# Pairwise products of 4096 rows: when, and through which queue, the input is loaded

## The chip, the cores and the metric

The kernel runs on 1 core of one Trainium2 chip. Its time is device microseconds of one execution; the number given is the median of several. Five engines take part: VectorE (DVE in the profile), ScalarE (ACT), GpSimd (POOL), SyncE (SP) and TensorE (PE, here only a relay for a semaphore). Each has its own stream of instructions. Transfers between HBM and the on-chip memory run on 16 DMA engines; SyncE and GpSimd each have a queue that feeds them (q1 and q0 in the profile).

## What is computed

The input has 4096 rows of 256 numbers. For each row, all products of two of its elements with the first index not above the second are written out in order: 256 x 257 / 2 = 32896 numbers per row.

```python
d = inputs.shape[1]
dot = jnp.einsum('bi,bj->bij', inputs, inputs)
iu, ju = jnp.triu_indices(d)
return dot[:, iu, ju]
```

All in 32-bit floats: 4.19 MB are read and 538.97 MB written.

## The kernel before

The 128 partitions hold 32 input rows each. Two rows of every partition make a *unit* (`each` = 512 floats, 2 KB per partition, 256 KB in all); there are 16 units, all kept in the tile `x`. A *pass* covers two units, so a loop of 8 passes (`h` from 0 to 7) covers the input. Each pass has six *pieces* (`p` from 0 to 5), three for each unit. A piece is a third of the 32896 output columns for the two rows of a unit: about 10.9 thousand floats by 2 rows by 128 partitions, 10944 or 11008 KB.

Pieces are computed into two places, `o0` and `o1`, in turn. VectorE copies the unit to `xv` and `xp` (line 209) and multiplies one element by the elements that follow it (line 230); GpSimd does the same for its share of the piece (line 315). The shares are cut so that GpSimd's part is estimated at 19.4 us. When both are done, SyncE issues one store of the whole piece (line 343). Its landing frees the place (`free0`, `free1`), VectorE waits for that before it starts the next piece there (lines 217 and 220), and it lets GpSimd start with `go`. So two stores can be in the queue: while one is being written, the piece for the other place is computed.

The first two pieces (`AHEAD`) are computed ahead of the loop by VectorE and ScalarE, and GpSimd does nothing then. Piece 0 goes out in five stores of growing size (`FIRST`), which raise `head`; TensorE waits for all five and then raises `free0`. VectorE and GpSimd then wait for the remaining early loads, and enter the loop with piece 2. At the end of a pass each engine computes the first two pieces of the next one.

The input comes in two ways. `NEAR` (line 383) are three loads of SyncE over all partitions: unit 0, units 1 and 2, and units 3 to 7. VectorE and ScalarE start when the first has landed. `LATE` are the units 8 to 15, by GpSimd in two turns: in pass 2 the units 8, 9, 12 and 13, in pass 3 the units 10, 11, 14 and 15. The issues stand in GpSimd's stream behind its part of pieces 2 and 3 (`late`, lines 281 and 274), five loads after each, and behind piece 5 it waits for them, with one drain after the second turn.

A late load takes 14 partitions, every ninth one (`COMB` = 9), and two runs of 4 KB in each; a last one takes the two partitions that are left. Between two loads stands a *mark*: a tiny load of 2 rows to a tile `marks` that nobody reads. One mark of 5 rows (`FORE`) comes first, and one of 14 (`AFT`) ends a turn. A load of 14 rows and a mark of 2 take 16 rows together.

Of the kernel before, what the change touches and what calls it, by code (L numbers as in the profile page):

```python
# [12 lines left out]
P = 128  # L13
# [1 line left out]
REPEAT = 2  # L15
PIECES = 3
EDGE = 32
NEAR = [(0, 1), (1, 3), (3, 8)]
LATE = {2: (8, 12), 3: (10, 14)}
TURNS = {2: range(5), 3: range(5, 10), 5: ()}  # L20
UNITS = 2
COMB = 9
FORE, AFT = 5, 14
MARK = 64
PLACES = 2
SETS = 2
# [39 lines left out]
def interleave(block: list) -> list:  # L66


    sets, k = [], 0
    for left in range(SETS, 0, -1):  # L70
        share = -(-len(vector_ops(block[k:])) // left)
        end = k
        while end < len(block) and len(vector_ops(block[k : end + 1])) <= share:
            end += 1
        if left == 1:
            end = len(block)
        sets.append(vector_ops(block[k:end]))
        k = end
    order, last = [], {}
    for step in range(max(map(len, sets))):  # L80
        for s, ops in enumerate(sets):
            if step < len(ops):
                order.append((*ops[step], last.get(s)))
                last[s] = len(order) - 1 if ops[step][1] == 2 else None
    return order


def schedule(order: list) -> dict:


    waits = {}
    for k, (*_, before) in enumerate(order):
        if before is not None and before > max(waits.values(), default=-1):
            waits[k] = max(before, k - 2)
    return waits
# [21 lines left out]
def window(ap: bass.AP, free: list) -> bass.AP:  # L117
    return bass.AP(ap.tensor, ap.offset, [list(ap.ap[0]), *free])
# [3 lines left out]
def kernel(  # L122
# [15 lines left out]
    nc = tc.nc  # L138
    n, d = x.shape
    width = out.shape[1]  # L140
    each, groups = REPEAT * d, n // (P * REPEAT)
# [8 lines left out]
    x_in = x.rearrange("(p g) d -> p (g d)", p=P)  # L150
# [5 lines left out]
    xt = pool.tile([P, passes, rounds * each], F32, name="x")  # L156
    xv = pool.tile([P, each + 1], F32, name="xv")
    marks = pool.tile([P, 2, 2 * MARK], F32, name="marks")
# [4 lines left out]
    def semaphore(name: str):  # L163
        return ctx.enter_context(nc.semaphore(name))

    free = [semaphore(f"free{k}") for k in range(PLACES)]
    head, v_done, a_done, go = (semaphore(s) for s in ("head", "v_done", "a_done", "go"))
    loaded = [semaphore(f"loaded{k}") for k in range(len(NEAR))]
    far, marked = semaphore("far"), semaphore("marked")
    teeth = P // COMB  # L170
    rest = P - COMB * teeth

    def take(engine, sem, value: int):
        engine.wait_ge(sem, value).then_inc(sem, -value)  # L174
# [7 lines left out]
    def blocks(p: int, ahead: bool):  # L182

        lo, hi = spans[p % PIECES]
        cuts = [lo, *(FIRST if ahead and p == 0 else []), hi]
        for a, b in zip(cuts, cuts[1:]):
            block = runs(d, a, b)
            if ahead:
                k = split(block)
                yield a - lo, b - lo, block[:k], block[k:], lo  # L190
            else:
                k = next(k for k in range(len(block)) if gpsimd_time(block[k:]) <= BUDGET * 1e3)
                yield a - lo, b - lo, block[k:], block[:k], lo
# [73 lines left out]
                else:  # L267
                    nc.scalar.sem_inc(a_done, 1)

    flat = xt.rearrange("p h d -> p (h d)")  # L270

    def mark(lo: int, hi: int):
        of = window(x_in[lo:hi], [[2 * MARK, 2], [1, MARK]])
        nc.gpsimd.dma_start(marks[lo:hi, :, :MARK], of).then_inc(marked, 16)  # L274

    def load_late(units: tuple, k: int):
        one, two = units
        rows = slice(k, k + COMB * (teeth - 1) + 1, COMB) if k < COMB else slice(P - rest, P)
        free = [[(two - one) * each, 2], [1, UNITS * each]]
        to, of = (window(ap[rows, one * each :], free) for ap in (flat, x_in))  # L280
        nc.gpsimd.dma_start(to, of).then_inc(far, 16)  # L281
        if k < COMB:
            mark(FORE + rest * k, FORE + rest * (k + 1))
        else:
            mark(FORE + rest * k, FORE + rest * k + AFT)

    def late(h, p: int):
        for turn, (when, units) in enumerate(LATE.items()):
            with nc.gpsimd.If(h == when):
                if TURNS[p]:  # L290
                    for k in TURNS[p]:
                        if turn == k == 0:
                            mark(0, FORE)
                        load_late(units, k)
                else:
                    nc.gpsimd.wait_ge(far, 16 * (turn + 1) * (COMB + 1))
                    nc.gpsimd.wait_ge(marked, 16 * ((turn + 1) * (COMB + 1) + 1))
                    if turn + 1 == len(LATE):
                        nc.gpsimd.drain()

    def gpsimd(h, pieces: range, ahead: bool):

        done = turns = 0
        for p in () if ahead else pieces:
            place = places[p % PLACES]
            ((_, _, block, _, lo),) = blocks(p, False)
            turns += 1
            nc.gpsimd.wait_ge(go, turns)
            order = interleave(block)
            waits = schedule(order)  # L310
            counted = {len(order) - 1, *waits.values()}
            number = {k: done + 1 + c for c, k in enumerate(sorted(counted))}
            for k, ((i, j, at, length), m, _) in enumerate(order):
                at -= lo
                ins = nc.gpsimd.tensor_tensor(  # L315
                    place[:, :, at : at + m * length],
                    window(xv[:, j:], [[d, REPEAT], [1, m], [1, length]]),
                    window(xv[:, i:], [[d, REPEAT], [1, m], [0, length]]),
                    ALU.mult,
                )  # L320
                if k in waits:
                    ins._wait_ge(g_own, number[waits[k]])
                if k in counted:
                    ins.then_inc(g_own, 1)
            done += len(counted)
            nc.gpsimd.wait_ge(g_own, done).then_inc(g_done, 1)  # L326
            if p in TURNS:
                late(h, p)
            if (p + 1) % PIECES == 0:
                nc.gpsimd.sem_inc(x_read, 1)  # L330
        if turns:
            nc.gpsimd.sem_inc(g_own, -done)
            nc.gpsimd.sem_inc(go, -turns)
# [14 lines left out]
    def settle(done: int, ahead: bool = False):  # L348
        nc.sync.sem_inc(v_done, -done)
        nc.sync.sem_inc(a_done if ahead else g_done, -done)  # L350

    def all_pieces(engine, pieces_of):
        done = pieces_of(0, range(AHEAD), True)
        if engine is nc.vector:
            nc.vector.sem_inc(v_own, -done)
        elif engine is nc.sync:
            settle(done, True)
        if engine is not nc.sync:
            for sem in loaded[1:]:
                engine.wait_ge(sem, 16)  # L360
        kind = engine.engine
        with nc.Fori(
            0,
            passes,
            engines=OrderedEngineSet([kind]),
            head_slot={kind: 0} if engine is not nc.sync else {},
        ) as h:
            done = pieces_of(h, range(AHEAD, PASS), False)
            with engine.If(h < passes - 1):
                nxt = nc.s_assert_within(h + 1, 0, passes - 1)  # L370
                if engine is nc.vector:
                    nc.vector.sem_inc(v_own, -vector(nxt, range(AHEAD), False, done))
                elif engine is nc.sync:
                    settle(sync(nxt, range(AHEAD), False, done) - done)
                else:
                    pieces_of(nxt, range(AHEAD), False)
            if engine is nc.sync:
                settle(done)
        if engine is nc.vector:
            nc.vector.sem_inc(v_own, -done)  # L380

    for (lo, hi), sem in zip(NEAR, loaded):
        nc.sync.dma_start(flat[:, lo * each : hi * each], x_in[:, lo * each : hi * each]).then_inc(sem, 16)

    nc.vector.memset(xv[:, each:], 0.0)  # L385
    for engine in (nc.vector, nc.scalar):
        engine.wait_ge(loaded[0], 16)
# [4 lines left out]
    for engine, pieces_of in ((nc.vector, vector), (nc.gpsimd, gpsimd), (nc.sync, sync)):  # L392
        all_pieces(engine, pieces_of)
# [32 lines left out]
```

## Time and profile before

| | |
|---|---|
| median of 3 runs | 1269.0 us (1268.93 to 1269.31) |
| the profiled execution | 1268.93 us, its span 1267.1 us |
| VectorE busy | 795.2 us (63% of the span) |
| GpSimd busy | 789.6 us (62%) |
| ScalarE busy | 29.2 us (2%) |
| bytes moved | 543.26 MB, mean 429 GB/s |
| GpSimd's late loads | 20, issued from 367.6 to 558.9 us, 23.6 us of GpSimd with their 21 marks |
| such a load of 112 KB, issue to landing | 22.4 us in the median, 48.3 us for the last ones |
| a store of 10944 KB, issue to landing | 33.8 us in the median |
| start of VectorE's first copy | 3.66 us |
| piece 1 enters SyncE's queue | about 37 us |
| VectorE and GpSimd start piece 2 | 41.88 us |

The profile shows one execution. Its span runs from the first instruction to the last. For the DMA engines it gives the share of time in which they moved packets, as a mean of the 16, by stretches. In a stretch that is not much longer than a packet this share jitters, and can be above 1, since a packet is put to the stretch in which it starts. The trace also holds a record of each packet: its start, its duration, its size and its queue, though not the number of its engine.

### The profile page before, as it was taken

How to read it: one execution, taken by the hardware profiler on the slowest of the kernel's cores; microseconds unless marked ns; L12 is line 12 of the kernel's file. 1: busy time of each engine (PE TensorE's matmuls, PEld its weight loads, DVE VectorE, ACT ScalarE, POOL GpSimd, SP SyncE). 2: the span in 40 equal slices, each digit the busy share in tenths (PEclk: the TensorE clock that was granted, in tenths of full speed). 3: DMA queues.
4: the chain of work that ended last, by engine and by line, in shares of the span. 5: the costliest groups of instructions: out<-in, count | busy, mean ns of one | idle time of the engine just before them, and what ended most of it. 6: DMA issues, size and time to landing. Idle time of an engine off the chain costs nothing. (4 is left out here: it accounts for less than half of the span.)

```text
span 1267.1 us, 3025 instructions
## 1 busy us (share of the span) xinstructions
DVE 795.2 (63%) x1197; ACT 29.2 (2%) x79; POOL 789.6 (62%) x1073
## 2 busy tenths in 40 slices
DVE  8856846667475674756747666486655866468560
ACT  8000000000000000000000000000000000000000
POOL 0467664776578765787655775567656675566750
DMA  9999999999999999999999999999999999999998
GB/s 380 394 444 420 442 439 424 441 423 442 422 436 431 430 426 440 428 426 432 437 429 439 429 435 430 436 442 424 438 429 437 439 427 439 426 438 431 435 440 349
DMA packets 16215, 543.26 MB, mean 429 GB/s; under 512 B 1931, under 2 KB 2000, under 8 KB 3280
## 3 DMA queue, kind: packets, MB, share of 16 engines
q1 hardware_dynamic: 14576, 541.07, 99.0%
q0 software_dynamic: 1632, 2.14, 0.5%
q14 instruction: 7, 0.06, 0.0%
HBM read 4.23 MB, written 538.97 MB: 429 GB/s over the span
## 5 line engine op out<-in xcount | busy, mean ns | idle before, releaser
L230 DVE TENSOR_TENSOR o<-xv,xp 128x512 f32<-128x512 f32 (+61 forms) x1164 | 777.2, 749 | 422.8 <-DMA out_dram<-o 304.7
L315 POOL TENSOR_TENSOR o<-xv 128x292 f32<-128x292 f32 (+60 forms) x1028 | 765.9, 785 | 435.3 <-DVEq L217 297.3
L256 ACT ACTIVATE o<-x 128x253 f32<-128x253 f32 (+38 forms) x78 | 28.0, 453 | 0.0
L209 DVE COPY xv<-x 128x512 f32 (+1 forms) x16 | 6.8, 428 | 14.4 <-DVEq L174 11.9
L281 POOL DMA_DIRECT2D x<-in_r_inputs_dram x20 | 11.5, 576 | 2.4 <-POOL o L315 2.4
L274 POOL DMA_DIRECT2D marks<-in_r_inputs_dram x21 | 12.1, 576 | 0.9 <-POOL o L315 0.9
L209 DVE COPY xp<-x 128x512 f32 (+1 forms) x16 | 11.1, 695 | 0.6
L256 ACT ACT_TABLE_LOAD x1 | 1.3, 1283 | 3.7 <-DMA x<-in_r_inputs_dram 3.7
L385 DVE MEMSET xv<- 128x1 f32 x1 | 0.1, 59 | 1.0 <-SPq L161 1.0
L413 POOL MEMSET const-float32-0.0<- 128x1 f32 x1 | 0.1, 98 | 0.3 <-issue 0.3
L413 POOL MEMSET const-bfloat16-1.0<- 128x1 bf16 x1 | 0.1, 101 | 0.0
L413 POOL MEMSET const-uint8-127<- 128x1 uint8 x1 | 0.1, 101 | 0.0
L413 POOL MEMSET const-float32-1.0<- 128x1 f32 x1 | 0.1, 98 | 0.0
## 6 DMA issues: line engine op xcount, KB each, us to landing
out_dram<-o SPq DMA_DIRECT2D x31, 10944.0 KB, 33.8
out_dram<-o SPq DMA_DIRECT2D x16, 11008.0 KB, 31.7
out_dram<-o SPq DMA_DIRECT2D x1, 4544.0 KB, 15.3
out_dram<-o SPq DMA_DIRECT2D x1, 2816.0 KB, 10.9
out_dram<-o SPq DMA_DIRECT2D x1, 2048.0 KB, 8.4
x<-in_r_inputs_dram POOLq DMA_DIRECT2D x18, 112.0 KB, 22.4
x<-in_r_inputs_dram SPq DMA_DIRECT2D x1, 1280.0 KB, 8.3
out_dram<-o SPq DMA_DIRECT2D x1, 1024.0 KB, 5.9
```

What stands on the lines that cost most here:

```text
L209: ins = nc.vector.tensor_copy(to, x_of(h, p // PIECES))
L230: ins = nc.vector.tensor_tensor(place[:, :, at : at + m * length], window(xv[:, j:], [[d, REPEAT], [1, m], [1, length]]), window(xp[:, i:] ...
L256: nc.scalar.activation(places[p][:, r, at - lo : at - lo + length], xa[:, r * d + j : r * d + j + length], AF.Copy, scale=xa[:, r * d + i ...
L274: nc.gpsimd.dma_start(marks[lo:hi, :, :MARK], of).then_inc(marked, 16)
L281: nc.gpsimd.dma_start(to, of).then_inc(far, 16)
L315: ins = nc.gpsimd.tensor_tensor(place[:, :, at : at + m * length], window(xv[:, j:], [[d, REPEAT], [1, m], [1, length]]), window(xv[:, i:] ...
L385: nc.vector.memset(xv[:, each:], 0.0)
L413: nc = _bacc.Bacc("TRN2", target_bir_lowering=False, num_devices=1)
```

## The change

The loads are divided anew, and all are issued ahead of the loop. SyncE loads unit 0, units 1 and 2, and unit 9. GpSimd loads the units 3 to 8 and 10 to 15, with runs of 12 KB in place of 4 KB, again 14 partitions at a time, in one sequence of 10 loads and 10 marks at the very start of its stream. The mark of 14 rows is gone. Ahead of its loop GpSimd waits for SyncE's second and third load, for all its loads and all its marks, and drains once; VectorE waits for SyncE's second and third load and for all of GpSimd's loads. The branches and waits for late loads inside the loop are gone. SyncE has no wait for GpSimd's loads.

```diff
-NEAR = [(0, 1), (1, 3), (3, 8)]
-LATE = {2: (8, 12), 3: (10, 14)}
-TURNS = {2: range(5), 3: range(5, 10), 5: ()}
-UNITS = 2
+NEAR = [(0, 1), (1, 3), (9, 10)]
+FAR = [3, 10, 6]
 COMB = 9
-FORE, AFT = 5, 14
+FORE = 5
...
+    landings = [*((sem, 16) for sem in loaded), (far, 16 * (COMB + 1)), (marked, 16 * (COMB + 1))]
...
-    def load_late(units: tuple, k: int):
-        one, two = units
-        rows = slice(k, k + COMB * (teeth - 1) + 1, COMB) if k < COMB else slice(P - rest, P)
-        free = [[(two - one) * each, 2], [1, UNITS * each]]
-        to, of = (window(ap[rows, one * each :], free) for ap in (flat, x_in))
-        nc.gpsimd.dma_start(to, of).then_inc(far, 16)
-        if k < COMB:
-            mark(FORE + rest * k, FORE + rest * (k + 1))
-        else:
-            mark(FORE + rest * k, FORE + rest * k + AFT)
-
-    def late(h, p: int):
-        for turn, (when, units) in enumerate(LATE.items()):
-            with nc.gpsimd.If(h == when):
-                if TURNS[p]:
-                    for k in TURNS[p]:
-                        if turn == k == 0:
-                            mark(0, FORE)
-                        load_late(units, k)
-                else:
-                    nc.gpsimd.wait_ge(far, 16 * (turn + 1) * (COMB + 1))
-                    nc.gpsimd.wait_ge(marked, 16 * ((turn + 1) * (COMB + 1) + 1))
-                    if turn + 1 == len(LATE):
-                        nc.gpsimd.drain()
...
-            if p in TURNS:
-                late(h, p)
...
         if engine is not nc.sync:
-            for sem in loaded[1:]:
-                engine.wait_ge(sem, 16)
+            for sem, count in landings[1:4]:
+                engine.wait_ge(sem, count)
+        if engine is nc.gpsimd:
+            engine.wait_ge(marked, landings[-1][1])
+            engine.drain()
...
+    def load_far(rows: slice):
+        one, two, units = FAR
+        free = [[(two - one) * each, 2], [1, units * each]]
+        to, of = (window(ap[rows, one * each :], free) for ap in (flat, x_in))
+        nc.gpsimd.dma_start(to, of).then_inc(far, 16)
...
+    mark(0, FORE)
+    for k in range(COMB):
+        load_far(slice(k, k + COMB * (teeth - 1) + 1, COMB))
+        mark(FORE + rest * k, FORE + rest * (k + 1))
+    load_far(slice(P - rest, P))
```

`mark` itself is unchanged and stands ahead of the loop now.

More of the change, by code (lines that the diff above doesn't have):

```diff
@@ L268, in scalar @@
                     nc.scalar.sem_inc(a_done, 1)
[L270 to L274, printed above, removed]
-    def load_late(units: tuple, k: int):
-        one, two = units
-        rows = slice(k, k + COMB * (teeth - 1) + 1, COMB) if k < COMB else slice(P - rest, P)
-        free = [[(two - one) * each, 2], [1, UNITS * each]]
-        to, of = (window(ap[rows, one * each :], free) for ap in (flat, x_in))
-        nc.gpsimd.dma_start(to, of).then_inc(far, 16)
-        if k < COMB:
-            mark(FORE + rest * k, FORE + rest * (k + 1))
-        else:
-            mark(FORE + rest * k, FORE + rest * k + AFT)
-    def late(h, p: int):
-        for turn, (when, units) in enumerate(LATE.items()):
-            with nc.gpsimd.If(h == when):
-                if TURNS[p]:
-                    for k in TURNS[p]:
-                        if turn == k == 0:
-                            mark(0, FORE)
-                        load_late(units, k)
-                else:
-                    nc.gpsimd.wait_ge(far, 16 * (turn + 1) * (COMB + 1))
-                    nc.gpsimd.wait_ge(marked, 16 * ((turn + 1) * (COMB + 1) + 1))
-                    if turn + 1 == len(LATE):
-                        nc.gpsimd.drain()
     def gpsimd(h, pieces: range, ahead: bool):
@@ L380, in all_pieces, with mark @@
             nc.vector.sem_inc(v_own, -done)
+    flat = xt.rearrange("p h d -> p (h d)")
     for (lo, hi), sem in zip(NEAR, loaded):
         nc.sync.dma_start(flat[:, lo * each : hi * each], x_in[:, lo * each : hi * each]).then_inc(sem, 16)
+    def load_far(rows: slice):
[3 more added lines that the diff above has]
+        nc.gpsimd.dma_start(to, of).then_inc(far, 16)
+    def mark(lo: int, hi: int):
+        of = window(x_in[lo:hi], [[2 * MARK, 2], [1, MARK]])
+        nc.gpsimd.dma_start(marks[lo:hi, :, :MARK], of).then_inc(marked, 16)
+    mark(0, FORE)
[3 more added lines that the diff above has]
+    load_far(slice(P - rest, P))
     nc.vector.memset(xv[:, each:], 0.0)
```

## The prediction

> **What bounds the kernel now.** I read the DMA queues first, then the busy time by stretches, then the timeline where a piece starts, then the chain of waits. The queues:
>
> ```profile
> q1 hardware_dynamic: 14576, 541.07, 99.0%
> q0 software_dynamic: 1632, 2.14, 0.5%
> ```
>
> SyncE's queue alone fills 99.0% of the 16 DMA engines, and 539 of its 541 MB are the output. VectorE (63% busy) and GpSimd (62%) are not the bound. So the time can only change where the DMA engines have nothing to do, where a transfer costs more than its bytes, or where the engines do not finish together. Two stretches show all the idle time there is: the start (the rows are: stretch, its length, busy VectorE, ScalarE, GpSimd, clock, DMA share, GB/s),
>
> ```profile
> 0.00:5.00 5.00, 1.33 (x4) 1.27 (x1) 0.20 (x4) 1.00 0.58 199
> 5.00:10.00 5.00, 5.00 (x8) 4.99 (x15) 0.00 (x0) 1.00 0.95 370
> 10.00:30.00 20.00, 20.00 (x28) 20.00 (x58) 0.00 (x0) 1.00 1.01 429
> 30.00:34.50 4.50, 4.50 (x7) 2.98 (x9) 0.00 (x0) 1.00 0.94 404
> 34.50:37.20 2.70, 2.32 (x5) 0.00 (x0) 0.00 (x0) 1.00 0.08 34
> 37.20:45.00 7.80, 3.12 (x6) 0.00 (x0) 3.13 (x7) 1.00 1.04 444
> ```
>
> and the end:
>
> ```profile
> 1260.00:1261.00 1.00, 0.00 (x0) 0.00 (x0) 0.00 (x0) 1.00 0.61 264
> 1261.00:1262.00 1.00, 0.00 (x0) 0.00 (x0) 0.00 (x0) 1.00 0.31 132
> 1262.00:1263.00 1.00, 0.00 (x0) 0.00 (x0) 0.00 (x0) 1.00 0.11 44
> 1263.00:1264.00 1.00, 0.00 (x0) 0.00 (x0) 0.00 (x0) 1.00 0.10 44
> ```
>
> At 34.5 the first output piece (piece 0) and the loads have gone, and piece 1 enters the queue only when VectorE has finished it, at 37.2: 2.7 us at a share of 0.08, so 2.5 us lost. From 37.2 on the share is 1.00. At the end a share counts packets by their start, and one packet of a store takes 1.63 us in the packet records: 0.11 x 1.00 x 16 / 1.63 = 1 packet starts in 1262 to 1263 and 1 in 1263 to 1264. So one or two engines still carry a packet or two when the rest have finished. The packet records say it exactly: eight engines end the last store at 1261.2 to 1261.3, six at 1262.2 to 1262.9, one at 1263.5 and one at 1265.5. That last one is the time. (In these records a packet starts within 10 ns of the end of the one before it on its engine, so an engine can be followed.)
>
> VectorE starts most pieces when the slowest of the 16 engines has landed the store that held the place. These starts are therefore a beat of the slowest engine:
>
> ```profile
> 66.11 13.72 DVE L230 TENSOR_TENSOR o<-xv,xp 128x1024 f32<-128x1024 f32 x14 [2.72 <-DMA out_dram<-o]
> ...
> 351.42 19.99 DVE L230 TENSOR_TENSOR o<-xv,xp 128x260 f32<-128x260 f32 x39 [11.10 <-DMA out_dram<-o]
> ...
> 457.07 13.18 DVE L230 TENSOR_TENSOR o<-xv,xp 128x1024 f32<-128x1024 f32 x13 [3.31 <-DVEq L174]
> ```
>
> From 66.11 to 351.42 are 11 pieces, 25.94 us each. The next four, in which GpSimd issues its first turn of late loads, end at 457.07: 105.65 us, where four quiet beats are 103.76.
>
> **The change, part by part.** Durations are of the profiled execution: span 1267.1, time 1268.93, 0.07 us under the median 1269.0.
>
> *GpSimd's late loads leave the loop.* 20 loads and 21 marks go (0.57 us each, 23.6 us of GpSimd), and the branches around them. GpSimd waits for VectorE 297.3 us in 32 waits, so its own time is worth nothing; the DMA engines' time is. Turn one cost the beat 105.65 - 103.76 = 1.9 us; turn two, with the starts 535.56 and 642.87, cost 107.31 - 103.76 = 3.6. Sum **-5.4 us**.
>
> *The same bytes come at the start.* SyncE's third load shrinks from 1280 to 256 KB; GpSimd now loads 3072 KB in place of 2048, before everything. A mark of 5 rows and then 14 rows and 2 rows in turn keep the loads to 14 of 16 engines, as in the late turns. An engine that is loaded carries 64 + 219 = 283 KB at the start in place of 128; at 432 GB/s / 16 = 27 GB/s the 155 KB more take 5.9 us. Most engines finish piece 0 at 34.4 now, three at 35.9 to 36.3 (packet records). Added to that: 34.4 + 5.9 = 40.3 at best, 36.3 + 5.9 + 1.1 = 43.3 at worst. The 1.1 is the cost of switching between the queues; two stretches of 26 us of the first late turn, from 364 on, moved 424 and 421 GB/s instead of 432: (8 + 11) x 26 / 432. Piece 1 is in the queue from 37.2, so these engines lose no time but are 3.1 to 6.1 us late on it; its landing, 63.7 for most and 65.5 for one engine now, becomes 66.8 to 69.8 at the slowest. The beat pays +1.3 to +4.3. I take **+2.5**, a little under the middle, because the three stragglers follow SyncE's third load, which shrinks.
>
> *The two skipped engines.* They carry 64 KB in place of 128, finish piece 0 before 37.2, and wait there: their lead is not kept. In the packet records the one that ends at 1265.5 is a skipped engine. At the end of the second turn it is at 614.1, where 25.89 us per store (the pace of the undisturbed engines) from 63.7 gives 607.4. Of these 6.7 us 1.9 or 2.5 had built up before the first turn, so 4.2 to 4.8 came during the turns, and up to 1.6 of that is drift that also goes on without loads. Its own gain is 2.6 to 4.8, which agrees with -5.4 + 2.5 = -2.9.
>
> The Trainium skill ("DMA: Bandwidth & Descriptors", Latency and other measured facts) says that two of the engines are usually slower, with GpSimd's descriptor rings as a best guess, and that this belongs to GpSimd's transfers alone. By that rule the drift would vanish with the loads, and the time would fall to about 1263.5. The trace differs: between 668.60 and 1214.01 GpSimd issues no transfer, and one engine goes from level with the others to 4.3 us behind.
>
> *The start of VectorE.* It begins at 3.66, when the 256 KB of unit 0 have landed. GpSimd's first load can be issued only after the mark (0.73 us), from about 1.7 on, when unit 0's packets run from 2.0 to 3.3. Bounds: 0, and 0.9 (two load packets, by the 0.385 us of a 10 KB packet about 0.46 each, ahead of it on an engine). I take **+0.2**: nearer to the first. What starts later here shifts piece 1 and all after it. VectorE is not slowed by the issuing itself: its 128x484 operation takes 656 ns beside GpSimd's DMA issues and 656 without.
>
> *The new waits.* GpSimd's wait and drain stand ahead of its loop, where it sits idle until 41.87 anyhow; behind them is only its first piece. 20 issues from about 1 us on are done by 12.5. VectorE waits for the same loads after piece 1, at 36.8; behind that wait is piece 2, which starts at 41.88 now because of 5.1 us that no wait explains. Nothing if the loads land by 41; the rival below prices it. SyncE's queue is unchanged but for the smaller load, and its missing waits at the end cost nothing in either version.
>
> Sum: -5.4 + 2.5 + 0.2 = **-2.7 us**: 1268.93 - 2.7 + 0.07 = **1266.3**. About 0.2% (2.5 us) is what can be told from no change here, so this lies on the edge of it.
>
> **The rivals.**
> 1. *The skipped engine keeps its delay.* If its 4.2 to 4.8 us of the turns were drift and not the loads, only its share of marks and completion writes goes (some 0.03 us for each of 22 marks and 0.01 for each of 40 completions: 1.0). Then 1269.0 - 1.0 + 0.2 = 1268.2, no change. For it: the drift in the quiet stretch. Against: there it is 0.16 us per store, too little for 4 us in 10 stores.
> 2. *The loads land too late (slower).* GpSimd's loads now take 22.4 us to land, the worst 48.3, since each of their packets takes turns with a store's. From the last issue at 12.5, 22.4 gives 35, hidden; 48.3 gives 60.8, and VectorE's piece 2 starts there, its store enters 20.3 us later at 81, and the engines, dry from 66 on, lose 15: 1269 - 3 + 15 = 1281. It decides from a landing at about 45 on, and at 50 the time is 1271. Against: at the start the store packets are 2 to 18 KB, not 43. A weaker form: piece 0 lands at 46 or later, with the same effect through its place.
> 3. *No more drift*: 1263.5, the loaded engines alone set the end.
>
> **How the numbers follow.** The forecast has 0.45 (1265 to 1267.5; two thirds of it beyond 0.2%), rival 1 0.27, rival 2 0.20 (some 1268 to 1281), rival 3 0.08. Faster: 0.30 + 0.08 = 0.38. Slower: most of rival 2, and a late start of VectorE, 0.22. The rest, 0.40, is within 0.2%. The range, 1263.5 to 1271.5, leaves out the upper half of rival 2 and the edge of rival 3.
>
> **What would show it.** The gap at 34.5 to 37.2 is filled; the share of the software queue stands in the first 25 us alone; four beats around 351 and 535 are 103.8; the starts of pieces 2 and 3 come at 42 to 43 and 67 to 69; the last engine is less than 4 us behind the mass. Wrong would be: piece 2 after 45, VectorE starting after 4.2, DMA shares under 1.00 after 60 us, or a tail longer than now.

## The result, and the profile after

The changed kernel takes 1266.05 us (median of 21 runs, 1265.84 to 1266.76) where the kernel before took 1269.21 beside it: a ratio of 0.9976, with a 95% interval from 0.9969 to 0.9983. That is 3.2 us less; 2.7 were forecast. The profiled execution took 1265.95 us, its span is 1264.1 instead of 1267.1.

The queues of the changed kernel, from the page:

```profile
q1 hardware_dynamic: 14576, 540.02, 98.9%
q0 software_dynamic: 800, 3.16, 0.7%
```

GpSimd's queue now carries 3.16 MB in place of 2.14, in half as many packets. The start of the changed kernel by stretches (length, busy VectorE, ScalarE and GpSimd, clock, DMA share, GB/s):

```profile
0.00:5.00 5.00, 1.14 (x3) 1.04 (x1) 3.57 (x10) 1.00 0.57 184
5.00:10.00 5.00, 4.97 (x9) 4.99 (x14) 5.00 (x10) 1.00 0.95 344
10.00:30.00 20.00, 20.00 (x27) 20.00 (x57) 3.02 (x6) 1.00 1.02 414
30.00:34.50 4.50, 4.50 (x7) 3.21 (x10) 0.00 (x0) 1.00 1.02 436
34.50:37.20 2.70, 2.56 (x6) 0.00 (x0) 0.00 (x0) 1.00 0.96 411
```

The hole between 34.5 and 37.2 is filled: its share is 0.96 and was 0.08. GpSimd issues until 13 us, where it had nothing else to do. The starts of pieces, in the timeline of the changed kernel (start, duration, engine, line, what, and in brackets the idle time before and what ended it):

```profile
3.89 0.43 DVE L208 COPY xv<-x 128x512 f32<-128x512 f32 x1 [2.80 <-DMA x<-in_r_inputs_dram]
...
42.99 19.99 DVE L229 TENSOR_TENSOR o<-xv,xp 128x260 f32<-128x260 f32 x39 [5.93 <-PEq L375]
...
353.59 19.99 DVE L229 TENSOR_TENSOR o<-xv,xp 128x260 f32<-128x260 f32 x39 [11.10 <-DMA out_dram<-o]
...
457.16 3.42 DVE L229 TENSOR_TENSOR o<-xv,xp 128x1024 f32<-128x1024 f32 x3 [4.18 <-DVEq L173]
```

VectorE starts 0.23 us later. Piece 2 starts 1.1 us later, and it now waits for TensorE's relay (line 375), that is for the landing of piece 0. From 353.59 to 457.16 four pieces take 103.57 us, where the same stretch with late loads took 105.65. The end of the changed kernel:

```profile
1256.00:1257.00 1.00, 0.00 (x0) 0.00 (x0) 0.00 (x0) 1.00 1.42 616
1257.00:1258.00 1.00, 0.00 (x0) 0.00 (x0) 0.00 (x0) 1.00 0.31 132
1258.00:1259.00 1.00, 0.00 (x0) 0.00 (x0) 0.00 (x0) 1.00 0.01 0
1259.00:1260.00 1.00, 0.00 (x0) 0.00 (x0) 0.00 (x0) 1.00 0.10 44
1260.00:1261.00 1.00, 0.00 (x0) 0.00 (x0) 0.00 (x0) 1.00 0.10 44
```

The last two rows hold one packet each (0.10 x 16 = 1.6 us, the length of one): a single engine is still writing. By the packet records the other fifteen finish between 1258.1 and 1259.0 and the last one at 1262.5.

### The profile page after: what moved, and what is told of

It reads as the page before. It is cut to its first block, busy times and chain, and to the rows that moved or that the text cites. A ratio compares the mean times of both kernels' runs of the same rounds, so it can differ in the third digit from the quotient of the medians.

```text
span 1264.1 us, 2954 instructions
## 1 busy us (share of the span) xinstructions
DVE 795.2 (63%) x1197; ACT 29.2 (2%) x79; POOL 777.5 (62%) x1052
## 3 DMA queue, kind: packets, MB, share of 16 engines
q0 software_dynamic: 800, 3.16, 0.7%
## 5 line engine op out<-in xcount | busy, mean ns | idle before, releaser
L363 POOL DMA_DIRECT2D marks<-in_r_inputs_dram x10 | 5.8, 584 | 1.2 <-SPq L159 1.2
L359 POOL DMA_DIRECT2D x<-in_r_inputs_dram x10 | 5.6, 560 | 0.0
## 6 DMA issues: line engine op xcount, KB each, us to landing
out_dram<-o SPq DMA_DIRECT2D x31, 10944.0 KB, 33.8
```

## Theory and rivals for the experiments

The theory: one engine of the skipped pair sets the end. From the entry of piece 1 on it is never idle, so only what lies on that engine counts, and the loads at the start, which skip it, cost next to nothing. The first rival is the sum as the prediction wrote it, by the beat of whichever engine is slowest: the late loads are worth 5.4 us and the start takes 2.5 back. The second is that the slow engine belongs to GpSimd's transfers. The Trainium skill ("DMA: Bandwidth & Descriptors", Latency and other measured facts) calls two engines usually slower, gives GpSimd's descriptor rings as a best guess for the reason, and takes this to be specific to GpSimd's transfers.

## Experiments

Each kernel was timed beside the kernel before on the same chip. Where two experiments are compared, it is by their differences to that kernel; the changed kernel's is -3.2 us. The intervals of the ratios reach about 1 us to each side, so times alone cannot tell a few tenths of a microsecond between two kernels; there the packet records decide.

**No late loads in the kernel before.** The edit, with `x_of` also turned to unit 0 for every pass:

```diff
-            if p in TURNS:
-                late(h, p)
...
-        return xt[:, bass.ds(h, 1), q * each : (q + 1) * each].rearrange("p o d -> p (o d)")
+        return xt[:, 0:1, :each].rearrange("p o d -> p (o d)")
```

> The kernel before, with GpSimd's late loads and marks left out altogether; every unit is computed from unit 0, so the products of the other units are not the reference's. It prices the removal alone. By the sum of the prediction (the two turns cost the slowest engine's beat 5.4 us, and the start gives 2.5 back) the removal alone is worth -5.4: about 1263.8 us. By the theory that a skipped engine alone sets the end, and that it does not notice the loads at the start of the changed kernel, this kernel ends with the changed one: 1265.5 to 1266.3 us, with the late loads worth only about 3 us. By rival 1 (drift, not the loads) 1268.

Measured: 1265.50 us against 1268.92 of the kernel before, ratio 0.9973 (0.9962 to 0.9983). The late loads were worth 3.4 us (2.2 to 4.8 by the interval), not 5.4. This is where the theory put it.

**No GpSimd loads in the changed kernel.** The ten loads and ten marks at the start, and the waits for them, are left out; units are computed from unit 0 again.

```diff
-    mark(0, FORE)
-    for k in range(COMB):
-        load_far(slice(k, k + COMB * (teeth - 1) + 1, COMB))
-        mark(FORE + rest * k, FORE + rest * (k + 1))
-    load_far(slice(P - rest, P))
...
-            for sem, count in landings[1:4]:
+            for sem, count in landings[1:3]:
```

> The changed kernel without GpSimd's loads and marks at the start, all computed from unit 0 (the products of the other units are not the reference's). It prices the loads at the start. By the sum of the prediction it is 2.5 to 2.7 us faster than the changed kernel: 1263.4 us. By the theory that a skipped engine sets the end it is within 0.4 us of it, the 0.2 us of VectorE's earlier start being most of the difference: 1265.6 to 1266.1 us, with the other 14 engines on piece 1 some 6 us earlier than in the changed kernel.

Measured: 1265.48 against 1268.92, ratio 0.9972 (0.9962 to 0.9983). Both kernels without GpSimd's loads are 3.4 us under the kernel before, and the changed kernel is 3.2 under it. So 3.1 MB of loads at the start cost some 0.3 us. That is too little to be told by the times, but the records agree with it: without the loads VectorE starts at 3.58 us in place of 3.89, and piece 1 enters the queue at 36.87 in place of 37.19. So the later start alone accounts for it. The stretches of this run show what the loads fill:

```profile
30.00:34.50 4.50, 4.50 (x7) 2.90 (x9) 0.00 (x0) 1.00 0.91 392
34.50:37.20 2.70, 2.23 (x5) 0.00 (x0) 0.00 (x0) 1.00 0.00 0
37.20:45.00 7.80, 3.21 (x6) 0.00 (x0) 3.22 (x7) 1.00 1.04 444
```

All engines stand still from 34.5 to 37.2, with 1 MB loaded and not 4. Freeing fourteen engines of loads at the start gains nothing, since all sixteen wait for piece 1.

**Another pair skipped, in both kernels.** A first mark of 9 rows in place of 5 turns the sequence by four engines; the bytes stay the same.

```diff
-FORE = 5
+FORE = 9
```

> The changed kernel with the first mark of 9 rows in place of 5, so that the same loads skip another pair of engines. Theory: the two engines skipped so far end last, and a load of 219 KB (8 us) more at the start makes them enter piece 1 late, at 41 to 42 us in place of 37.5; all of that is found at the end: 1269.5 to 1271 us, and the tail (last engine behind the mass) grows from 4 to about 8 us or the mass comes later. If which pair is skipped does not matter, 1266 us.

```diff
-FORE, AFT = 5, 14
+FORE, AFT = 9, 14
```

> The kernel before with the first mark of 9 rows in place of 5, so that the late loads skip another pair of engines. Theory: from 37 us on the two engines skipped so far never idle, so each late load that they now carry is found at the end: 36 packets of 4 KB at 0.159 us are 5.7 us, 1273 to 1275 us. If the pair does not matter: 1269.

Measured: the changed kernel with the other pair takes 1268.76 us against 1268.92 of the kernel before (ratio 1.0000, 0.9991 to 1.0009), so 3.0 us of the gain, nearly all, is gone. The kernel before with the other pair takes 1272.46 against 1268.90 (ratio 1.0028, 1.0018 to 1.0039), 3.6 us more. Both are in the direction of the theory and below its numbers (1269.5 to 1271, and 1273 to 1275). In the packet records of the changed kernel's run the pair now skipped ends piece 0 at 36.9 and 37.1, and one engine still ends the last store 4.3 us behind the next one. Followed back, this engine lands piece 1 at 66.96 where the last engine of the changed kernel lands it at 64.13: 2.8 us later, and not the 3.5 to 4.5 that I had expected, and these 2.8 are found at the end (1265.33 against 1262.51). For the kernel before I had counted the whole of the packets that the slow engine takes over, and not what it stops paying as a skipped engine. Against the kernel without late loads the sequence costs 7.0 us when the slow engine carries it and 3.4 when it is skipped. That the marks are what a skipped engine pays for was not measured.

**No GpSimd transfers at all.** SyncE loads everything, in three loads.

```diff
-NEAR = [(0, 1), (1, 3), (9, 10)]
+NEAR = [(0, 1), (1, 3), (3, 16)]
```

(and GpSimd's loads, marks and their waits go, as above)

> The changed kernel with all 16 units loaded by SyncE over all engines (third load units 3 to 15, 3328 KB) and no transfer of GpSimd at all. Theory of the drift that belongs to an engine and not to GpSimd's transfers: one engine still ends about 4 us behind the mass; each engine carries 192 KB more at the start than a skipped one does, 7 us, so that piece 0 ends at 39 to 41 us and the time is 1 to 3 us over the changed kernel: 1267 to 1269 us. By the page's rule that the slow engines belong to GpSimd's descriptor rings: the tail shrinks to under 1.5 us and the time falls to 1264 or less.

Measured: 1267.48 against 1268.92, ratio 0.9989 (0.9980 to 0.9998): 1.7 us slower than the changed kernel, as the theory had it. Its queues and its end:

```profile
q1 hardware_dynamic: 14576, 543.17, 99.4%
q14 instruction: 7, 0.06, 0.0%
```

```profile
1259.00:1260.00 1.00, 0.00 (x0) 0.00 (x0) 0.00 (x0) 1.00 0.11 44
1260.00:1261.00 1.00, 0.00 (x0) 0.00 (x0) 0.00 (x0) 1.00 0.10 44
1261.00:1262.00 1.00, 0.00 (x0) 0.00 (x0) 0.00 (x0) 1.00 0.00 0
1262.00:1263.00 1.00, 0.00 (x0) 0.00 (x0) 0.00 (x0) 1.00 0.10 44
```

There is no software queue, and still a single engine ends at 1264.0 while fifteen are done at 1259.6 to 1259.7. The slow engine does not belong to GpSimd's transfers, so the skill's best guess does not hold here. Skipping it is worth these 1.7 us: it lands piece 1 at 65.60 here, where it is 64.13 in the changed kernel.

**Piece 1 stored in two parts.** The skipped engines end piece 0 at 36.3 and 36.7 in the changed kernel and get piece 1 at about 37.5.

```diff
-        cuts = [lo, *(FIRST if ahead and p == 0 else []), hi]
+        cuts = [lo, *(FIRST if ahead and p == 0 else [lo + c for c in SECOND] if ahead else []), hi]
...
-                store.then_inc(free[p % PLACES] if len(parts) == 1 else head, 16)
+                store.then_inc(free[p % PLACES] if len(parts) == 1 else (head, second)[p], 16)
...
+    take(nc.tensor, second, 16 * (len(SECOND) + 1))
+    nc.tensor.sem_inc(free[1], 16)
```

> The changed kernel with piece 1 stored in two parts (after 5504 of its columns), so that the engines need not wait for all of it. Theory: the skipped engines, which end piece 0 at 36.3 and 36.7 us and get piece 1 at about 37.5, no longer wait: 0.8 to 1.2 us less, 1264.9 to 1265.4 us. If their wait there is not on the path: 1266.

Measured: 1267.49 against 1268.90, ratio 0.9989 (0.9980 to 0.9998), 1.7 us slower than the changed kernel; 0.8 to 1.2 faster was expected. The timeline of this run shows why:

```profile
44.63 19.99 DVE L231 TENSOR_TENSOR o<-xv,xp 128x260 f32<-128x260 f32 x39 [7.01 <-issue]
...
64.88 0.39 SPq L311 DMA_DIRECT2D out_dram<-o  x1
```

VectorE starts piece 2 at 44.63 in place of 42.99, after 7.0 us that no wait explains, and the store of piece 2 enters at 64.88 instead of 63.23. The skipped engines did move ahead: they end piece 1 at 63.3 and 65.1, where it was 64.1 and 65.8. But the first then has nothing to write until piece 2 comes, and ends that at 91.8 where it was 90.2. What the split won at 37 us was lost at 63.

**The same, and less for the skipped engines to load.**

```diff
-NEAR = [(0, 1), (1, 3), (9, 10)]
-FAR = [3, 10, 6]
+NEAR = [(0, 1), (1, 2)]
+FAR = [2, 9, 7]
```

> As the one before, and units 2 and 9 are loaded by GpSimd as well (SyncE loads units 0 and 1, GpSimd the units 2 to 8 and 9 to 15, runs of 14 KB), so that the skipped engines carry 32 KB in place of 64 at the start. Theory: a skipped engine saves another 2 packets-worth per partition, 0.8 to 1.2 us, and the loaded engines, which end 4 us earlier, have room for it: 1264.0 to 1264.6 us. If the wait is elsewhere: 1265 or more.

Measured: 1270.05 against 1268.90, ratio 1.0008 (0.9999 to 1.0018), 4.3 us slower than the changed kernel. The skipped engines end piece 1 at 61.6 and 61.9, the loaded ones end piece 0 at 42.1 to 45.0, VectorE starts piece 2 at 45.69, and its store enters at 65.93: both skipped engines stand still for some 4 us and end piece 2 at 93.0. But this is not what sets the end. Followed back through the packet records, the engine that ends last at 1267.28 is not one of them: it lands piece 1 at 68.92 and piece 2 at 94.97, so it is a loaded engine here, and it is 4.8 us later than in the changed kernel at piece 1 and at the end. GpSimd's units 2 to 15 lie side by side, and its packets are of 28 KB in place of 12 KB. Why the same sequence of rows then skips another pair was not tried. So this run says nothing on fewer loads for the slow engine; it shows once more that what this engine carries ahead of piece 1 is found at the end.

**VectorE done earlier with piece 1.** Nothing but the split between VectorE and ScalarE ahead of the loop changes.

```diff
-        scalar += REPEAT * (184 + 0.837 * block[k][3])
+        scalar += REPEAT * 0.86 * (184 + 0.837 * block[k][3])
```

> The changed kernel with ScalarE's estimated cost in the split of the first two pieces multiplied by 0.86: VectorE hands it two more of the runs, so that VectorE ends piece 1 about 1.3 us earlier (at 35.7 in place of 37.1) and ScalarE later (at about 35). Nothing else changes. Theory: the skipped engines, which end piece 0 at 36.3 and 36.7 us, find piece 1 in the queue in place of waiting until 37.5 for it, and one of them sets the end: 0.8 to 1.2 us less, 1264.9 to 1265.3 us. Unlike the split store it does not put VectorE's start of piece 2 later. If the gap at 37 us is not on the path: 1266.

Measured: 1265.86 against 1269.03, ratio 0.9975 (0.9965 to 0.9985): 3.17 us under the kernel before, as the changed kernel is with 3.16. No gain can be told. VectorE ended piece 1 at 35.3 as planned, and the two skipped engines ended it at 63.5 and 65.0, 0.6 and 0.8 us earlier. The store of piece 2 enters at about 63.0, held by the loaded engines' landing of piece 0. One skipped engine ends piece 2 at 90.0 in place of 90.2, the other at 91.0 in place of 91.7, and the last engine of the run ends at 1262.2 in place of 1262.5.

**A store cut so that the slow engine writes less.** In pass 5 SyncE stores 112 partitions of piece 2 and GpSimd the last 16, skipping the pair; a second run skips another pair.

```diff
+                    with nc.sync.If(h == WHEN):
+                        store = nc.sync.dma_start(to[:ROWS], place[:ROWS, :, lo:hi])
...
+                with nc.gpsimd.If(h == WHEN):
+                    lo, hi = spans[p % PIECES]
+                    take(nc.gpsimd, ready, 1)
+                    for a, b in ((ROWS, ROWS + 14), (P - 2, P - 1), (P - 1, P)):
...
+                        nc.gpsimd.dma_start(to, place[a:b, :, : hi - lo]).then_inc(rest_in, 16)
+                        if a == ROWS:
+                            mark(40, 42)
```

> The changed kernel, in which one store of 48 (piece 2 of pass 5) is cut: SyncE stores 112 partitions of it, seven to each engine, and GpSimd the other 16, of which 14 in one transfer that skips the same two engines as the loads, and one each in two more (4 engines write one packet of 1.6 us more). Theory that one slow engine of the skipped pair sets the end and all others wait for it: it writes two packets of 1.62 us less, so the time falls by up to 3.2 us, less what the others then show: 1262.8 to 1264.5 us. If all engines bound the time together: 1266, or over it by the extra transfers.

> As the run before, but a mark of 6 rows in place of 14 ahead of it turns the sequence by 8 engines, so that the cut store skips another pair; the loads at the start are the same. Theory: the slow engine writes as much as ever, the others have 4 us of room: 1265.5 to 1266.5 us. If the gain of the run before came from cutting a store at all: as there.

Measured: 1284.23 against 1269.20 (ratio 1.0110, 1.0095 to 1.0125), and 1294.81 (1.0195, 1.0181 to 1.0208). Both say nothing on the theory, because the cut store itself was slow. The DMA issues of the first of the two runs (queue, count, KB each, us to landing), and below them two stretches of it:

```profile
out_dram<-o SPq DMA_DIRECT2D x1, 9632.0 KB, 53.2
...
out_dram<-o POOLq DMA_DIRECT2D x1, 1204.0 KB, 21.3
```

```profile
832.00:858.00 26.00, 20.98 (x32) 0.00 (x0) 16.75 (x24) 1.00 1.05 360
858.00:884.00 26.00, 2.94 (x5) 0.00 (x0) 7.15 (x6) 1.00 0.96 306
```

A store of 9632 KB took 53.2 us to land where 10944 KB take 33.8, and for two stretches the engines were busy and moved 360 and 306 GB/s instead of 432. In the packet records GpSimd's 32 packets of 43 KB took 1.6 to 7.7 us each, where 1.62 us is usual. All 32 read the same 16 partitions, from many engines at a time; that this is the reason was not tried. So a version that takes bytes off the slow engine is still open, and no kernel here is clearly faster than the changed one.

**The engine that ends last, followed through the runs.** By the times at which the 16 engines finish each store, the one that ends last can be followed back through the packet records. Here are the changed kernel and seven variants, with the time at which this engine finishes (lands) its part of piece 2, and its end:

| kernel | it lands piece 2 | it ends |
|---|---|---|
| no GpSimd loads in the changed kernel | 89.81 us | 1262.08 us |
| no late loads in the kernel before | 89.82 | 1262.09 |
| VectorE done earlier with piece 1 | 89.98 | 1262.20 |
| the changed kernel | 90.21 | 1262.51 |
| no GpSimd transfers at all | 91.66 | 1263.97 |
| piece 1 in two parts | 91.83 | 1264.08 |
| changed kernel, another pair skipped | 93.02 | 1265.33 |
| two parts, and units 2 and 9 by GpSimd | 94.97 | 1267.28 |

In each row 1172.2 to 1172.3 us lie between the two, 26.05 us a store, where the other engines need 25.88. In all of them its lag grows by the same amounts, store by store and within 0.1 us. So it never waits behind piece 2, whatever the other fifteen do, and the time at which it lands piece 2 is the whole difference between these executions. In the kernel before, the stores from piece 13 to piece 22, beside the late loads, take this engine 263.8 us, and 260.6 without them: 3.2 us.

## Why the prediction was right, point by point

- **The time.** 1266.3 was forecast, 1266.05 measured; the direction and the size held. That they are so close is luck: the two large terms of the sum were both too large, and their errors cancelled.
- **The late loads leave the loop: -5.4.** This step failed in its size. With these loads alone taken out the kernel gained 3.4. The error is in the beat: before a turn of late loads the slowest engine is a skipped one, behind the turn it is another, so the beat's loss is not one that a single engine pays. The other account, of the skipped engine's own delay in the turns, gave 2.6 to 4.8, and holds: followed through both turns, this engine loses 3.2.
- **The same bytes come at the start: +2.5.** Also wrong in size: 0.3, with VectorE's later start in it. What was predicted for the loaded engines came out: they end piece 0 at 40.6 to 42.2 (40.3 to 43.3 forecast), and the slowest landing of piece 1 is at 68.0 (66.8 to 69.8). But none of them ends last. The beat of the slowest engine does pay at the start, but the end does not go by that beat. The errors, of 2.0 us in the first step and 2.4 in this one and the start of VectorE together, cancelled. The mechanism that the runs show is the one that stood beside the sum as a check.
- **The two skipped engines.** Their lead was said not to be kept, as they end piece 0 before 37.2 and wait. They do, at 36.3 and 36.7, so they wait only about 1 us. In the two kernels without GpSimd's loads all engines wait 2.5 us and more, and the last one still enters piece 1 at nearly the same time, so these are hardly faster.
- **The start of VectorE: +0.2.** Measured 0.23 (3.66 to 3.89).
- **The new waits: nothing.** VectorE's start of piece 2 at 42.99 is ended by TensorE's relay, so by the landing of piece 0, and not by the wait for the loads. That wait is over long before. The DMA issues of the changed kernel (queue, count, KB each, us to landing):

```profile
x<-in_r_inputs_dram POOLq DMA_DIRECT2D x9, 336.0 KB, 6.3
```

These loads land in 6.3 us in the median, where those in the loop took 22.4, and the last packet of GpSimd's queue ends at 22.2 us. Rival 2 did not occur. The reason given, that the store packets beside these loads are small at the start, fits the two times, but no run tried it apart.
- **Rival 1** (the delay is drift, not the loads) was priced at 1268.2. Removing the loads gave 3.4 us, so it falls; but drift is there without any late loads: 0.17 us a store in every run of the table, as 26.05 against 25.88.
- **Rival 3** (no more drift, 1263.5) falls with the run without GpSimd's transfers, and so does the skill's rule behind it as far as this kernel goes.
- **What would show it.** The filled hole, the beats (103.57 against 103.8), the starts of pieces 2 and 3 (42.99 and 68.53) came as written. The tail did not: the last engine is 4.3 us behind the mass (1262.5 against 1258.2), and "less than 4" was expected.

## What to carry to other kernels

When the DMA engines are the bound and one of them ends last, as here, a transfer costs what it takes from that engine, not its bytes over the mean rate. Loads that skip that engine were nearly free at the start (0.3 us for 3.1 MB), and the same skipping is worth 3.0 us against skipping another pair. And before two slowdowns are added up, ask whether they lie on the same engine: the beat of "whichever is slowest" mixes engines, and its losses do not add.

## What the runs showed that I had not expected

- The tail, from the earliest engine's end to the last one's, is nearly the same in all runs but the two with a cut store: 4.3 to 4.4 us, whatever was loaded when. In the changed kernel the fifteen others bunch together in the last stores (1180.1 to 1181.4 for piece 44, counted from 0), and the gap before that landing is 26.6 us where 25.9 is usual, so the earliest of them have waited. The reading that fits is that the two places cap the lag: a store can enter only about 21 us after the slow engine landed the one two before it, so the lag can't grow beyond about 25.9 - 21, some 5 us. No run varied the number of places, so this is argued and not shown.
- VectorE's pause on entering its loop grew with what the engines carried at that time: 5.05 us in the two runs without GpSimd's loads, 7.0 with piece 1 in two parts and 7.3 with all loads by SyncE, in each case with no wait to explain it. One instruction fetch of 8 KB, in the queue for instructions, falls into that time in the packet records (at 39.8 to 42.6 us). That it is this fetch which VectorE waits for was not tested.
- Why one engine is slow stays open. It is not GpSimd's transfers. The kernel before and the changed one both skip it: skipping another pair cost 3.6 and 3.0 us. The runs of the table with a recorded chip come from three chips, and the lag grows alike on all three.
